# A fifth tile of source rows by matmul in one chunk of twelve

## The chip, the core and the metric

The kernel runs on one NeuronCore of a Trainium2 chip. A core has five engines that run their own instruction streams and meet at semaphores: TensorE (PE, matmuls and, separately shown, their weight loads PEld), VectorE (DVE), ScalarE (ACT), GpSimd (POOL) and SyncE (SP). SP, ACT and POOL also issue DMAs, each on queues of its own. The metric is the device time of one execution in microseconds; less is better.

## What is computed

A graph layer over 12500 nodes of 32 features and 400000 edges sorted by target. Node features are normalised and rectified; each edge takes its source's row, its target's row and its own 32 attributes through a small two-layer network; each node takes the maximum over its incoming edges.

```python
def _L0_gnn_ref(x, edge_index, edge_attr, W1, b1, W2, b2):
    rol, col = (edge_index[0], edge_index[1])
    e_feat = jnp.concatenate([x[rol], x[col], edge_attr], axis=-1)
    h = jax.nn.relu(e_feat @ W1 + b1)
    v = h @ W2 + b2
    x_cand = jax.ops.segment_max(v, col, num_segments=num_nodes)
    return jnp.maximum(x_cand, x[:, -v.shape[-1]:])

h = jnp.maximum(_layernorm(x, axis=-1), 0.0)
x = x + _L0_gnn_ref(h, edge_index, edge_attr_32, W1, b1, W2, b2)
```

## The kernel before

**Tiling.** The edges are cut into four stripes, each stripe into 196 chunks of 512 edges. A chunk is thus 4 x 512 edges, held as 16 groups of 128 source rows (K = 16). The main loop (L530) takes two chunks per turn, c and c + 1; while it finishes these it fetches the source rows of a = c + 2 and b = c + 3. One turn is called a pair below. On PE a pair starts with the matmuls `ph<-ht`, which multiply the transposed source rows of c and c + 1 by the first weights.

**Two ways to a source row.** Of the 16 groups of a chunk, 12 are gathered: `gather` (L148) issues one indirect DMA per group of 128 rows on POOL, out of `h_d` in memory, into a buffer `gh` that holds three groups; there are 24 such buffers, four to a chunk. The other four groups (MM = 4), in every chunk but the last, are picked by matmul out of a copy of all nodes kept on the core:

- The 98 nodes that each partition holds are cut into A1 = 7 groups of A0 = 14. `hs` holds each node's features in two parts, whose sum is the value.
- An edge's source index becomes a *key* (which partition and which group of 14) and a *place* within the 14. The keys are worked out once, at the start, from `src_mm` (L390 to L392) and written to `key_d` in memory. `load_keys` (L187) brings them back, broadcast to all partitions as `kb`, for two chunks by one DMA of 256 KB on ACT's queue.
- `one_hots` (L202, VectorE, five of the seven groups) and `one_hots_act` (L210, ScalarE, the other two) turn the keys into one-hot columns `hot`. `mask_of` (L219) makes the mask that selects the place.
- `tile(c, m)` (L227) does one group of 128 edges: 14 matmuls of 128 x 128 by 448 columns (7 groups, two parts each, L238) into a bank of PSUM `pv`, then on VectorE a multiply with the mask (L242) and a maximum over the 14 (L243) into `gm`. Two banks are called `pv`, and the second layer of the network uses the same two.

`to_features` (L245) transposes rows, gathered or picked, into `ht`: parts 0 to 3 take the four gathered buffers (L256), part J = 4 the four picked groups (L259).

**Order.** The order of the instructions on SP, PE, VectorE and ScalarE is that of the program text; an engine does not pass a waiting instruction. POOL's gathers wait only for a free buffer. A turn runs on PE as: `tile(a,0)`, `ph<-ht`, `tile(a,1)`, `tile(a,2)`, `ph<-ea` (edge attributes), the second layer into two `pv` banks (L569), `ph<-of` (target rows), the leaving matmuls of the chunk before (L486), `tile(a,3)`, the transposes of `leave_1` (L476), `tile(b,0)`, `leave_2` (L486), `tile(b,1)`, `leave_1`, `tile(b,2)`, `tile(b,3)`. [...] On VectorE the two scans of the turn (L576), which make the running maximum over edges of one target, stand just ahead of `tile(a,3)`'s multiply.

**Loads.** At the head of a turn the DMAs for later turns are issued. `load_keys(a + 2)` comes first. Then `load(k)` (L437) for k = c + 4 and c + 5; where k is a multiple of LOAD = 4 it brings four chunks at once: `ea` (1 MB, SP's queue), `db` (1 MB, target indices, ACT's queue) and `pb` (512 KB, penalties, ACT's queue, L445). On ACT these issues stand behind the last ScalarE work of the turn before (`wo`, L490) and ahead of `hid` (L552). Every so often `load_block` follows with `di` and `ends`.

## Time and profile before

| | |
|---|---|
| median of 12 runs | 3053.06 us (3049.39 to 3059.16) |
| the profiled execution | 3044.69 us, of which the span from the first to the last instruction is 3042.9 |
| matmuls of `tile` (L238) | 10920, 780 tiles of 14 |
| gathers (L154) | 2345, the first at 27.7 us, the last at 2995.9 |
| `ph<-ht`, first of the first and last pair | 86.9 and 2984.5 us |

The profile comes from one execution. A group line has the source line, engine, operation, tiles (`out<-in`) with shapes and count, then after the bar busy time in us, the mean ns of one, and the engine's idle time just ahead of them with what ended it. A timeline line has start, duration, engine, line, operation and tiles, and in brackets the idle time before it and its releaser. A wait line has who waited for whom, the total in us, how often, and the longest. A stretch line has the window, its length, the busy time of PE, PEld, VectorE, ScalarE and POOL, the granted clock of PE as a share of full, and the DMA engines' share and GB/s. A queue line has packets, MB and share of the DMA engines; q10 is ACT's queue. Matmuls are pipelined and their ends are modelled, so a busy PE is not PE at its peak, and of two runs of matmuls the distance between starts tells more than the durations.

### The profile page before, as it was taken

How to read it: one execution, taken by the hardware profiler on the slowest of the kernel's cores; microseconds unless marked ns; L12 is line 12 of the kernel's file. 1: busy time of each engine (PE TensorE's matmuls, PEld its weight loads, DVE VectorE, ACT ScalarE, POOL GpSimd, SP SyncE). 2: the span in 40 equal slices, each digit the busy share in tenths (PEclk: the TensorE clock that was granted, in tenths of full speed). 3: DMA queues.
4: the chain of work that ended last, by engine and by line, in shares of the span. 5: the costliest groups of instructions: out<-in, count | busy, mean ns of one | idle time of the engine just before them, and what ended most of it. 6: DMA issues, size and time to landing. Idle time of an engine off the chain costs nothing. (4 is left out here: it accounts for less than half of the span.)

```text
span 3042.9 us, 58825 instructions
## 1 busy us (share of the span) xinstructions
PE 2958.6 (97%) x21189; PEld 2322.5 (76%) x21189; DVE 2244.4 (74%) x3869; ACT 1089.1 (36%) x1795; POOL 2255.2 (74%) x2376
## 2 busy tenths in 40 slices
PE   5999999999999999999999999999999999999995
PEld 4677787777878787777787777777777877777773
DVE  6577777777777777777777777777777777777775
ACT  4242433333343433333333333333333333333331
POOL 6777777777777777777777777777777777777774
PEclk9899999999999999999999999999999999999998
DMA  6332233233323322332233223322322332233322
GB/s 246 73 85 64 62 82 78 62 65 83 73 59 83 76 63 66 79 75 65 61 82 78 59 67 85 70 63 65 86 71 59 70 84 68 63 67 84 67 58 71
DMA packets 194678, 229.58 MB, mean 75 GB/s; under 512 B 118333, under 2 KB 158797, under 8 KB 181582
## 3 DMA queue, kind: packets, MB, share of 16 engines
q10 hardware_dynamic: 32580, 110.55, 12.0%
q1 hardware_dynamic: 86762, 76.67, 10.4%
q0 software_dynamic: 75040, 38.57, 8.7%
q8 instruction: 167, 2.74, 0.4%
q14 instruction: 129, 1.06, 0.1%
HBM read 211.68 MB, written 13.85 MB: 74 GB/s over the span
## 5 line engine op out<-in xcount | busy, mean ns | idle before, releaser
L154 POOL DMA_INDIRECT gh<-h_d,src_i x2345 | 2235.1, 953 | 746.5 <-issue 532.4
L238 PE MATMUL pv<-hs,hot 128*128 128x448 f32 x10920 | 2358.1, 371 | 7.8 <-DVE sm L576 7.5
L238 PEld LDWEIGHTS pv<-hs,hot 128*128 128x128 f32 x10920 | 2014.5, 188 | 270.3 <-issue 70.8
L242 DVE TENSOR_TENSOR one<-pv,mask 128x448 f32<-128x448 f32 x780 | 483.3, 620 | 685.6 <-PE pv L238 685.0
L552 ACT ACTIVATE hid<-ph,wt 128x512 f32<-128x512 f32 x392 | 237.3, 689 | 1254.5 <-PE ph L500 1189.2
L207 DVE TENSOR_TENSOR hot<-kb,consts 128x1536 fp32r<-128x1536 f16 (+2 forms) x388 | 565.8, 1458 | 0.0
L243 DVE TENSOR_REDUCE gm<-one 128x32 f32<-128x448 f32 x780 | 483.7, 620 | 26.8
L217 ACT ACTIVATE hot<-away,ones 128x512 fp32r<-128x512 f32 x392 | 283.7, 724 | 244.2 <-issue 234.5
L216 ACT ACTIVATE away<-kb,key_n 128x512 f32<-128x512 f16 x392 | 277.9, 709 | 0.0
L576 DVE TENSOR_TENSOR_SCAN sm<-pb,sm,pv 128x512 f32<-128x512 bf16 x195 | 247.6, 1270 | 14.5 <-PE pv L569 4.2
L256 DVE STREAM_TRANSPOSE ht<-gh 128x96 f32<-128x96 f32 x782 | 210.3, 269 | 42.7 <-DMA gh<-h_d,src_i 42.1
L486 PEld LDWEIGHTS tr<-so,last 128*64 128x64 f32 x3136 | 107.6, 138 | 112.8 <-issue 77.9
L490 ACT ACTIVATE wo<-tr 128x64 f32<-128x64 f32 x196 | 43.8, 223 | 381.3 <-PE tr L486 352.6
L462 ACT ACTIVATE of<-db,below 128x512 f32<-128x512 int32 x196 | 141.8, 723 | 16.9 <-DMA db<-in_dst_ext 16.9
L463 ACT ACTIVATE of<-of,ones 128x512 f32<-128x512 f32 x196 | 142.0, 724 | 6.4
L486 PE MATMUL tr<-so,last 128*64 128x64 f32 x3136 | 134.8, 228 | 3.9 <-DVE so L478 3.9
L569 PE MATMUL pv<-hid,wt 64*32 64x512 f32 x1568 | 130.7, 601 | 5.0 <-DVE one L242 4.3
L468 DVE TENSOR_TENSOR last<-consts,at 128x512 f32<-128x512 f32 x196 | 129.9, 663 | 0.0
L478 DVE TENSOR_TENSOR so<-tr,wt 128x512 f32<-128x512 f32 x196 | 127.8, 652 | 2.1 <-PE tr L476 2.1
L500 PE MATMUL ph<-of,qw 32*64 32x512 f32 x1568 | 115.6, 619 | 13.9 <-DMA qw<-q_d 13.9
L476 PE MATMUL tr<-ident,sm 128*128 128x128 f32 x784 | 117.5, 272 | 1.5 <-DVE sm L576 0.8
L500 PE MATMUL ph<-ht,wt 32*64 32x512 f32 x1568 | 112.7, 613 | 0.2 <-DVE ht L262 0.2
(77 smaller groups left out, 552.7 us busy)
## 6 DMA issues: line engine op xcount, KB each, us to landing
ea<-in_edge_attr SPq DMA_DIRECT2D x49, 1024.0 KB
db<-in_dst_ext ACTq DMA_DIRECT2D x48, 1024.0 KB
gh<-h_d,src_i POOLq DMA_INDIRECT x2345
pb<-pen_d ACTq DMA_DIRECT2D x48, 512.0 KB
kb<-key_d ACTq DMA_DIRECT2D x95, 256.0 KB
qw<-q_d SPq DMA_DIRECT2D x784, 8.0 KB
top_d<-wo SPq DMA_DIRECT2D x784, 4.0 KB
top_d<-zero ACTq DMA_DIRECT2D x2, 1568.0 KB
```

The source lines that it names most:

```text
L154: nc.gpsimd.indirect_dma_start(out=parts[-1][:, i, :], out_offset=None, in_=h_d[:, :], in_offset=bass.IndirectOffsetOnAxis(ap=src_i[:, c, ...
L207: nc.vector.tensor_tensor(hot_of(c)[:, start:stop], keys[c][:, None, :].to_broadcast([P, n, MM * P]), key_ps[:, start:stop, None].to_broad ...
L216: nc.scalar.activation(away, keys[c], AF.Square, bias=key_n[:, k:k + 1])
L217: nc.scalar.activation(hot_of(c)[:, k], away, AF.Relu, bias=ones, scale=-1.0)
L238: nc.tensor.matmul(po, hot[:, k, e], hs[:, part, k].rearrange("p f a -> p (f a)"), start=(k == 0 and part == 0), stop=(k == A1 - 1 and par ...
L242: nc.vector.tensor_tensor(one, of_group, masks[c][:, m, None, :].to_broadcast([P, D, A0]), op=ALU.mult)
L243: nc.vector.tensor_reduce(mm_rows[c][:, m, :], one, axis=AX.X, op=ALU.max)
L256: nc.vector.transpose(ht[:, r].rearrange("p k e -> p (k e)"), gh[c][part][:, :r.stop - r.start].rearrange("p k f -> p (k f)"))
L486: nc.tensor.matmul(pw[g * 2 * W:(g + 1) * 2 * W], last[:, j, 2 * g:2 * g + 2].rearrange("p s w -> p (s w)"), so[:, j, g * 2 * D:(g + 1) * ...
L500: nc.tensor.matmul(ph[s][x * HID:(x + 1) * HID], w[g], e[g], start=start, stop=stop)
L552: nc.scalar.activation(hid[s], ph[s], AF.Relu, bias=b1c)
L576: nc.vector.tensor_tensor_scan(sm, loaded.pop(c + x)[2], pv[x], before, op0=ALU.add, op1=ALU.max)
```

## The change

`MORE = range(6, NCH - 12, 12)` names 15 chunks, 6, 18, ... 174. In these the group of rows K - MM - 1 = 11 is no longer gathered (11 gathers in place of 12, the fourth buffer `gh` holding two groups) but picked by matmul, as a fifth tile. It has keys of its own at the end of `key_d`, a load of its own on ACT's queue (`load_more`, 128 keys to 128 partitions, 32 KB), a one-hot of 7 x 128 columns made on VectorE alone (`hot_more`), a mask of its own, and a row buffer of its own. All chunks of `MORE` are even and so play the part of a. `load_more(a)` stands behind the loads at the head of the turn, `hot_more(a)` between the scans and `tile(a, 3)`, `tile_more(a)` behind the last gathered part's transpose. The matmuls and the two VectorE instructions of `tile` move into `pick`, which both kinds of tile call. `places` works out the fifth tiles' places once, in its first call.

```diff
+MORE = range(6, NCH - 12, 12)
...
+    place_m = const.tile([P, len(MORE)], F32, name="place_m")
...
+    def gathers(c):
+        return min(K - MM * (c in MMC) - (c in MORE), (SE - c * C) // D)
+
     def gather(c):
-        n = min(K - MM * (c in MMC), (SE - c * C) // D)
+        n = gathers(c)
...
     def places(start, stop):
 
-        se = src_i[:, MMC.start + start:MMC.start + stop, K - MM:]
-        pk = place_k.rearrange("p (c m) -> p c m", m=MM)[:, start:stop]
-        group(pk, se)
-        nc.vector.scalar_tensor_tensor(pk, pk, -float(A0), se, op0=ALU.mult, op1=ALU.add)
+        more = src_i[:, MORE.start:MORE.stop:MORE.step, K - MM - 1]
+        for pk, se in ((place_k.rearrange("p (c m) -> p c m", m=MM)[:, start:stop],
+                        src_i[:, MMC.start + start:MMC.start + stop, K - MM:]),
+                       (place_m, more))[:1 + (start == 0)]:
+            group(pk, se)
+            nc.vector.scalar_tensor_tensor(pk, pk, -float(A0), se, op0=ALU.mult, op1=ALU.add)
...
     def tile(c, m):
 
-        if c not in MMC:
-            return
-        if m == 0:
-            mm_rows[c] = early.tile([P, MM, D], F32, name="gm", bufs=6)
-        hot = hots[c]
-        e = slice(m * P, (m + 1) * P)
+        if c in MMC:
+            if m == 0:
+                mm_rows[c] = early.tile([P, MM, D], F32, name="gm", bufs=6)
+            pick(hots[c][:, :, m * P:(m + 1) * P], masks[c][:, m], mm_rows[c][:, m, :])
+
+    def load_more(c):
+        if c in MORE:
+            kb = early.tile([P, P], F16, name="kb_more", bufs=1)
+            nc.scalar.dma_start(kb, ap(key_d, (len(MMC) * MM + MORE.index(c)) * P, [[0, P], [1, P]]))
+            keys_more[c] = kb
+
+    def hot_more(c):
+        if c in MORE:
+            hot = early.tile([P, A1, P], F32R, name="hot_more", bufs=1)
+            nc.vector.tensor_tensor(hot, keys_more[c][:, None, :].to_broadcast([P, A1, P]),
+                                    key_ps[:, :, None].to_broadcast([P, A1, P]), op=ALU.is_equal)
+            mask = early.tile([P, A0], F32, name="mask_more", bufs=1)
+            k = MORE.index(c)
+            nc.vector.tensor_tensor(mask, place_ps, place_m[:, k:k + 1].to_broadcast([P, A0]), op=ALU.is_equal)
+            keys_more[c] = hot, mask
+
+    def tile_more(c):
+
+        if c in MORE:
+            rows = early.tile([P, D], F32, name="gm_more", bufs=1)
+            pick(*keys_more.pop(c), rows)
+            nc.vector.transpose(hts[c][:, K - MM - 1], rows)
+
+    def pick(hot, mask, rows):
         po = early_ps.tile([P, C], F32, name="pv", bufs=2)[:, :D * A0]
...
-                nc.tensor.matmul(po, hot[:, k, e], hs[:, part, k].rearrange("p f a -> p (f a)"),
+                nc.tensor.matmul(po, hot[:, k], hs[:, part, k].rearrange("p f a -> p (f a)"),
...
-        nc.vector.tensor_tensor(one, of_group, masks[c][:, m, None, :].to_broadcast([P, D, A0]), op=ALU.mult)
-        nc.vector.tensor_reduce(mm_rows[c][:, m, :], one, axis=AX.X, op=ALU.max)
+        nc.vector.tensor_tensor(one, of_group, mask[:, None, :].to_broadcast([P, D, A0]), op=ALU.mult)
+        nc.vector.tensor_reduce(rows, one, axis=AX.X, op=ALU.max)
...
-            nc.vector.transpose(ht[:, n:].rearrange("p k e -> p (k e)"),
+            nc.vector.transpose(ht[:, K - MM:].rearrange("p k e -> p (k e)"),
                                 mm_rows.pop(c).rearrange("p k f -> p (k f)"))
...
-        key = pool.tile([P, len(MMC) * MM], F32, name="key")
-        key16 = pool.tile([P, len(MMC) * MM], F16, name="key16")
+        key = pool.tile([P, len(MMC) * MM + len(MORE)], F32, name="key")
+        key16 = pool.tile([P, len(MMC) * MM + len(MORE)], F16, name="key16")
...
+            load_more(a)
             tile(a, 0)
             to_features(a, 0)
...
+            hot_more(a)
             tile(a, 3)
             one_hots_act(a + 2)
             to_features(a, 3)
+            tile_more(a)
             to_features(a, J)
```

`key_d`, `src_mm` and its tile `sp` grow by 15 x 128 keys; the host lays these behind the others.

More of the change, by code (lines that the diff above doesn't have):

```diff
@@ L94, in gnn_kernel @@
     top_d = [dram.tile([NP, D], F32, name=f"top_d{k}") for k in range(2)]
-    key_d = dram.tile([len(MMC) * MM * P], F16, name="key_d")
+    key_d = dram.tile([(len(MMC) * MM + len(MORE)) * P], F16, name="key_d")
     acc_d = dram.tile([NP, D], F32, name="acc_d")
@@ L171, in gnn_kernel @@
     hts = {}
+    keys_more = {}
     loaded_b, ats = {}, {}
@@ L251, in to_features @@
         ht = hts[c]
-        n = min(K - MM * (c in MMC), (SE - c * C) // D)
+        n = gathers(c)
         if part < J:
@@ L289, in gnn_kernel @@
     with tc.tile_pool(name="nodes", bufs=1) as pool, tc.tile_pool(name="nodes_ps", bufs=2, space=PSUM) as ps:
-        sp = pool.tile([P, len(MMC) * MM], I32, name="sp")
+        sp = pool.tile([P, len(MMC) * MM + len(MORE)], I32, name="sp")
         nc.scalar.dma_start(sp, src_mm)
@@ L725 @@
     sc = np.ascontiguousarray(sp.reshape(NS, NCH, K, D).transpose(1, 2, 0, 3).reshape(NCH, K, P))
-    sm = sc[MMC.start:MMC.stop, K - MM:]
+    sm = np.concatenate([sc[MMC.start:MMC.stop, K - MM:].reshape(-1),
+                         sc[MORE.start:MORE.stop:MORE.step, K - MM - 1].reshape(-1)])
     w1, w2 = np.asarray(L0_gnn_W1), np.asarray(L0_gnn_W2)
@@ L741 @@
         "src": np.ascontiguousarray(sc.transpose(2, 0, 1).reshape(P, NCH * K)),
-        "src_mm": np.ascontiguousarray(sm.reshape(P, len(MMC) * MM)),
+        "src_mm": sm.reshape(P, len(MMC) * MM + len(MORE)),
         "src_t": sp.reshape(NS, TS, P),
```

## The prediction

> **What bounds the kernel now.** I read the busy shares and the groups of instructions first.

> ```profile
> PE 2958.6 (97%) x21189; PEld 2322.5 (76%) x21189; DVE 2244.4 (74%) x3869; ACT 1089.1 (36%) x1795; POOL 2255.2 (74%) x2376
> ...
> L154 POOL DMA_INDIRECT gh<-h_d,src_i x2345 | 2235.1, 953 | 746.5 <-issue 532.4
> L238 PE MATMUL pv<-hs,hot 128*128 128x448 f32 x10920 | 2358.1, 371 | 7.8 <-DVE sm L576 7.5
> ```

> PE looks like the bound at 97%, POOL at 74% does not. But a gather of 953 ns is followed by a gap of 0.30 us "issue" nearly every time, so POOL is in truth never free: its 2235 us and its 746 us of gaps fill the span from the first gather to the last. Two engines are full, and the question is which one gives the pace, and when. For that I took the busy time by stretch, cut at the first matmul of a pair of chunks (`ph<-ht`): 32 pairs in the first row, 62 in the second.

> ```profile
> 153.10:1106.10 953.00, 953.00 (x6913) 754.76 (x6912) 722.49 (x1255) 348.26 (x576) 715.85 (x753) 1.00 0.32 72
> 1106.10:2984.50 1878.40, 1866.28 (x13393) 1464.04 (x13392) 1397.25 (x2413) 674.78 (x1116) 1413.93 (x1486) 1.00 0.30 70
> ```

> Up to 1106 us PE is busy all the time and a pair takes 953.0/32 = 29.78 us. After that a pair takes 1878.4/62 = 30.30 us and PE has holes. What VectorE waits for says why (200 to 1000 us, then 1100 to 2990 us):

> ```profile
> DVE one L242 <- PE pv L238: 181.7, 151, 1.9
> ...
> DVE one L242 <- PE pv L238: 416.1, 353, 2.6
> DVE ht L256 <- DMA gh<-h_d,src_i: 42.1, 54, 2.1
> ```

> Early it waits for matmuls alone; late it waits for gathers too. POOL starts ahead (some 30 us between a gather's end and the transpose that reads it), loses half a microsecond per pair to PE, and from 1106 us on the lead is used up. So **PE sets the first third and POOL the rest**, and they differ by only 0.52 us per pair. An edit that gives work from POOL to PE can gain at most what POOL costs over PE, 62 x 0.52 = 32 us.

> **The change, part by part.** There are 15 such chunks (6, 18, ... 174).

> *Gathers removed*: 15. One costs 1878.4/1486 = 1.264 us of POOL, so POOL has 19.0 us less. Six pairs now hold 143 gathers, 180.8 us of POOL, against 6 x 29.78 + 2.95 = 181.6 us of PE (the 2.95 follows). POOL no longer falls behind, the lead of 30 us is never used up, and the whole 32 us of waiting for gathers goes: **-32**.

> *Matmuls added*: 14 per tile. The rows below give 42 of them from 323.80 to the next matmul at 332.56, 2.92 us per tile, and a lone 14 from 320.47 to 323.44, 2.97; I take 2.95. Nothing hides them, since PE is the pace once POOL is quick enough: 15 x 2.95 = **+44.3**.

> *VectorE's part*: the one-hot of 7 x 128 = 896 elements. 1024 take 1182 ns and 1536 take 1726 (L207), so 1.06 ns an element and 1.05 us; mask below the 0.20 us of L222; multiply and reduce 0.62 each (L242, L243); a transpose of 32 columns under the 0.27 of L256. One-hot and mask (1.25) fall into the 1.90 us in which VectorE waits before the multiply at 346.40, the rest runs under the next matmuls as it does for other tiles: 0 while that cover holds. The four small instructions on `place_m` and the wider key are at most +0.8 us at the start, once.

> *The keys' load*: this is the part I give most weight. It is one DMA of 32 KB on ACT's queue, issued behind whatever `load(k)` put there. A fifth-tile chunk is a = 6 + 12i, so c = 4 + 12i, and there `load` of chunk c + 4 = 8 + 12i, a multiple of 4, puts db and pb (1.5 MB) on the same queue in the same iteration, every time. The timeline of one such pair before the change (c = 16), and what ACT's queue (q10) moved from 319 to 334, 334 to 344.5 and 344.5 to 349.3 us:

> ```profile
> 320.47 3.13 PE L238 MATMUL pv<-hs,hot 128*128 128x448 f32 x14
> 320.65 0.33 ACTq L192 DMA_DIRECT2D kb<-key_d  x1
> 321.01 0.56 ACTq L444 DMA_DIRECT2D db<-in_dst_ext  x1
> 321.67 0.51 ACTq L445 DMA_DIRECT2D pb<-pen_d  x1
> ...
> 323.80 8.83 PE L238 MATMUL pv<-hs,hot 128*128 128x448 f32 x42
> ...
> 332.56 1.11 PE L500 MATMUL ph<-ht,wt 32*64 32x512 f32 x16
> ...
> 341.86 2.64 DVE L576 TENSOR_TENSOR_SCAN sm<-pb,sm,pv 128x512 f32<-128x512 bf16 x2
> ...
> 343.25 3.12 PE L238 MATMUL pv<-hs,hot 128*128 128x448 f32 x14
> 346.00 0.56 PEld L476 LDWEIGHTS tr<-ident,sm 128*128 128x128 f32 x4
> ...
> 346.40 0.63 DVE L242 TENSOR_TENSOR one<-pv,mask 128x448 f32<-128x448 f32 x1 [1.90 <-PE pv L238]
> ```

> ```profile
> q10 hardware_dynamic: 223, 0.91, 22.5%
> ...
> q10 hardware_dynamic: 100, 0.59, 16.7%
> ...
> q10 hardware_dynamic: 85, 0.33, 17.0%
> ```

> 0.91 + 0.59 + 0.33 = 1.83 MB is the kb, db and pb issued near 321 us (1792 KB). They go in turn: by packet size, kb's end first, then db's, then pb's, the last at 349.2. The keys would be issued at 322.2 and stand behind pb. VectorE wants them when the scans end, at 344.5; they come after 349.2. Over the 15 pairs concerned, the queue's last packet of that load ends 14.0 to 18.7 us after the pair's first matmul, mean 16.7; the fourth tile's matmuls end 13.6 us after it. Add 0.4 us for the 32 KB (0.33 MB in 4.8 us is 69 KB per us), 1.05 for the one-hot, 0.1 to hand over: PE stands still for 16.7 + 1.55 - 13.6 = 4.65 us. Behind the waiting one-hot on VectorE are the mask, the fourth tile's multiply and reduce and everything after; behind the tile's first matmul on PE are the transposes of `leave_1` and tile (b,0). All of it moves together and none of it is made up, PE having no holes: 15 x 4.65 = **+70**. Bounds: all as the earliest (14.0) 29, all as the latest 100.

> *The clock*. PE has not stood still for that long since the start. There it did three times, 5.1, 9.3 and 3.46 us, and after each the granted clock was half for 6.8, 13.7 and 6.8 us; the last of them (the clock is the third column from the right):

> ```profile
> 85.40:99.00 13.60, 11.61 (x94) 7.17 (x92) 10.04 (x15) 8.38 (x13) 10.25 (x12) 1.00 0.46 137
> 99.00:105.90 6.90, 5.43 (x14) 3.06 (x14) 0.00 (x0) 0.00 (x0) 5.11 (x6) 0.51 0.41 105
> ```

> Holes up to 1.25 us later on left it at 1.00. 4.65 us is nearest to the 5.1 and 3.46. Half clock for 6.8 us, about 1 of it in the hole itself, makes matmuls slower by 1.7 to 1.8 times, a loss of 2.5 us; I give each hole 8 chances in 10: 15 x 2.0 = **+30**. Bounds 0 and 46 (every hole, 3.1 each). [...]

> **Sum**: -32 + 44.3 + 0.8 + 70 + 30 = +113 us on the profiled execution's 3042.9 us of span (3044.7 with what lies around it). That execution is 8 us quicker than the median of the runs, 3053.06. I put the difference on the median: 3053 + 113 = **3166 us**. With the low bounds -32 + 44.3 + 0.8 + 29 = 42, so 3095; with the high ones 100 and 46, 159, so 3212.

> **Rivals.**
> 1. *Late keys, clock stays up*: 113 - 30 = 83, 3136 us. For it: only three cases of a drop, all at the start. Against it: the shortest of them was shorter than these holes.
> 2. *Keys in time*: the queue lets a small DMA pass, or its load ends earlier. Then -32 + 44.3 + 0.8 = 13, 3066 us. Against it: pb's packets follow db's in turn, and not one of the 15 loads ended before the scans.
> 3. *Faster*: PE takes the tile into its holes and POOL's 19.0 us come off, 3034 us. It decides if a tile costs PE under (32 - 19)/15 = 0.87 us with keys in time. Against it: 2.92 measured, and before 1106 us there are no holes.
> 4. *Worse*: holes long enough for 13.7 us of half clock, as after the 9.3 us. Another 3 us each, 45 in all, 3211 us.

> That the change doesn't do what it says I exclude: 11 gathers are issued, the fourth transpose covers rows 9 and 10, the tile's row 11.

> **Chances.** Forecast 0.65, rival 1 0.20, rival 2 0.08, rival 3 0.02, rival 4 0.05. The predicted time is the forecast's. The range 3095 to 3212 takes the bounds of the stall and the clock, holds rival 1 and half of rival 4, and leaves out rivals 2 and 3. A measurement here can tell 0.2%, 6 us, from no change. Faster by more: 0.02 (rival 3). Within it: 0.02, a rival 2 in which 7 of the 13 us are hidden. Slower: 0.96.

> **What would show it.** VectorE waits before the new one-hot for `kb_more`, about 15 times 5 us; holes of 4 to 5 us on PE before the fifth tile's matmuls and half clock after most of them; no waits of `ht` for gathers; pairs of 29.8 us without a fifth tile, and about 39 us with one. The forecast is wrong if the keys land before the scans end (then pairs of 32.7 us), or if VectorE still waits for gathers late in the run.

## The result, and the profile after

The changed kernel takes 3174.29 us in the median of 8 runs (3162.42 to 3178.70), the kernel before 3052.73 (34 runs): a ratio of 1.0393 with a 95% interval of 1.038 to 1.0406, some 121 us slower. The profiled execution has a span of 3161.1 us against 3042.9.

The page of the changed kernel: busy time by engine, the gathers, and the matmuls of the fifth tiles.

```profile
PE 3015.6 (95%) x21399; PEld 2386.1 (75%) x21399; DVE 2277.0 (72%) x3948; ACT 1089.1 (34%) x1795; POOL 2242.4 (71%) x2361
...
L159 POOL DMA_INDIRECT gh<-h_d,src_i x2330 | 2221.8, 954 | 804.3 <-issue 568.9
...
L269 PE MATMUL pv<-hs,hot_more 128*128 128x448 f32 x210 | 73.1, 526 | 74.7 <-DVE mask_more L255 74.7
```

There are 15 gathers fewer and 210 matmuls more. The new matmuls last 526 ns each where those of the other tiles last 371, and PE stands idle for 74.7 us ahead of them. VectorE's waits in the changed kernel:

```profile
DVE one L273 <- PE pv L269: 722.0, 555, 20.3
DVE hot_more L251 <- DMA kb_more<-key_d: 84.2, 15, 8.5
...
DVE ht L287 <- DMA gh<-h_d,src_i: 1.9, 2, 1.5
```

It waits for the fifth tile's keys 15 times out of 15, 84.2 us in all, 8.5 at most; the wait for gathers (42.1 us before) has shrunk to 1.9. One pair shows how that comes about. This is the timeline of the turn c = 16, with what ACT's queue moved from 332 to 344.4, 344.4 to 356.4 and 356.4 to 363 us.

```profile
332.60 0.33 ACTq L200 DMA_DIRECT2D kb<-key_d  x1
332.97 0.56 ACTq L475 DMA_DIRECT2D db<-in_dst_ext  x1
333.62 0.52 ACTq L476 DMA_DIRECT2D pb<-pen_d  x1
...
335.91 0.32 ACTq L245 DMA_DIRECT2D kb_more<-key_d  x1
...
353.78 2.64 DVE L608 TENSOR_TENSOR_SCAN sm<-pb,sm,pv 128x512 f32<-128x512 bf16 x2
...
355.17 3.11 PE L269 MATMUL pv<-hs,hot 128*128 128x448 f32 x14
...
363.00 1.09 DVE L251 TENSOR_TENSOR hot_more<-kb_more,consts 128x896 fp32r<-128x896 f16 x1 [6.57 <-DMA kb_more<-key_d]
364.00 0.17 DVE L255 TENSOR_TENSOR mask_more<-consts,place_m 128x14 f32<-128x14 f32 x1
...
364.23 5.19 PE L269 MATMUL pv<-hs,hot_more 128*128 128x448 f32 x14 [5.94 <-DVE mask_more L255]
...
369.26 0.60 PE L507 MATMUL tr<-ident,sm 128*128 128x128 f32 x4
```

```profile
q10 hardware_dynamic: 315, 0.80, 24.9%
...
q10 hardware_dynamic: 77, 0.57, 17.7%
...
q10 hardware_dynamic: 160, 0.50, 18.8%
```

0.80 + 0.57 + 0.50 = 1.87 MB is kb, db, pb and the 32 KB of keys. A DMA of 32 KB issued at 335.91 has landed at 363.00, 27 us later, when the last of the megabyte and a half ahead of it has gone. It doesn't stand behind them as a whole: going by size and time of the packets on q10 (256 bytes are the keys, 8 KB db, 4 KB pb), 96 of its 128 packets go from 336.9 to 338.1, while db's have only begun, and the last 32 from 361.0 to 362.2, with the last of pb's at 362.1. It is 96 and 32 in each of the 15 turns. The one-hot needs all of them. The scans are over at 356.42; VectorE idles 6.57 us, PE 5.94. Then 14 matmuls take 369.26 - 364.23 = 5.03 us (that is up to the next matmul's start) where the fourth tile's took some 2.95. The granted clock around the holes of two such pairs tells why (third column from the right):

```profile
362.00:368.80 6.80, 4.57 (x12) 4.13 (x13) 2.47 (x5) 0.00 (x0) 5.28 (x6) 0.50 0.11 20
...
2061.90:2065.30 3.40, 3.30 (x9) 2.98 (x10) 1.34 (x4) 0.00 (x0) 2.48 (x4) 0.50 0.10 18
```

All 15 holes (stretches in which PE stands still ahead of the fifth tile), 2.38 to 7.87 us long, were followed by half clock, for 3.4 us (8 of them), 6.8 (6) or 10.2 (1). Between the first and the last fifth tile the clock was full everywhere else.

### The profile page after: what moved, and what is told of

It is laid out like the page before. It is cut to its first block, busy times and chain, and to the rows that moved or that the text cites. A ratio compares the mean times of both kernels' runs of the same rounds, so it can differ in the third digit from the quotient of the medians.

```text
span 3161.1 us, 59320 instructions
## 1 busy us (share of the span) xinstructions
PE 3015.6 (95%) x21399; PEld 2386.1 (75%) x21399; DVE 2277.0 (72%) x3948; ACT 1089.1 (34%) x1795; POOL 2242.4 (71%) x2361
## 3 DMA queue, kind: packets, MB, share of 16 engines
q14 instruction: 130, 1.06, 0.1%
## 5 line engine op out<-in xcount | busy, mean ns | idle before, releaser
L269 PEld LDWEIGHTS pv<-hs,hot 128*128 128x128 f32 x10920 | 2016.6, 188 | 259.3 <-issue 70.6
L225 ACT ACTIVATE hot<-away,ones 128x512 fp32r<-128x512 f32 x392 | 283.3, 723 | 235.5 <-issue 225.8
L287 DVE STREAM_TRANSPOSE ht<-gh 128x96 f32<-128x96 f32 (+1 forms) x782 | 209.4, 268 | 1.9 <-DMA gh<-h_d,src_i 1.9
L269 PE MATMUL pv<-hs,hot_more 128*128 128x448 f32 x210 | 73.1, 526 | 74.7 <-DVE mask_more L255 74.7
L269 PEld LDWEIGHTS pv<-hs,hot_more 128*128 128x128 f32 x210 | 60.5, 296 | 86.5 <-issue 79.8
```

The source lines that it names most:

```text
L225: nc.scalar.activation(hot_of(c)[:, k], away, AF.Relu, bias=ones, scale=-1.0)
L269: nc.tensor.matmul(po, hot[:, k], hs[:, part, k].rearrange("p f a -> p (f a)"), start=(k == 0 and part == 0), stop=(k == A1 - 1 and part = ...
L287: nc.vector.transpose(ht[:, r].rearrange("p k e -> p (k e)"), gh[c][part][:, :r.stop - r.start].rearrange("p k f -> p (k f)"))
```

## The experiments

All use the changed kernel as their base. The kernels of a series were compared with the kernel before on the same chip. Chips differed: on three of six the kernel before took 3059 to 3064 us, on the other three 4146 to 4207. What the latter say is told in a part of its own; the numbers of the next three parts are from chips of the first kind.

**Keys ahead of the large loads.** One call moves up by a few lines.

```diff
             load_keys(a + 2)
+            load_more(a)
             for k in range(c + AHEAD, min(c + AHEAD + 2, NCH)):
                 load(k)
...
-            load_more(a)
             tile(a, 0)
```

> Keys issued ahead of db and pb, a third time, since both earlier series fell on chips where the kernel before takes over 4140 us. Where it takes about 3053 us: theory (late keys) 3066 us, no wait of the one-hot for its keys, no hole on PE ahead of the fifth tile; rival (the tile's own work) near 3174 us.

Measured: 3061.44 us against 3059.17 for the kernel before, 1.0008 (0.9996 to 1.0019). VectorE's waits in this kernel no longer have the keys, and PE starts the fifth tile without a hole:

```profile
DVE one L273 <- PE pv L269: 701.1, 571, 20.0
DVE acc L657 <- DMA part<-top_d: 10.8, 3, 8.5
...
DVE ht L287 <- DMA gh<-h_d,src_i: 2.8, 3, 1.5
```

```profile
347.01 2.64 DVE L608 TENSOR_TENSOR_SCAN sm<-pb,sm,pv 128x512 f32<-128x512 bf16 x2
349.57 1.06 DVE L251 TENSOR_TENSOR hot_more<-kb_more,consts 128x896 fp32r<-128x896 f16 x1
```

```profile
348.40 3.12 PE L269 MATMUL pv<-hs,hot 128*128 128x448 f32 x14
351.36 3.00 PE L269 MATMUL pv<-hs,hot_more 128*128 128x448 f32 x14
354.20 0.60 PE L507 MATMUL tr<-ident,sm 128*128 128x128 f32 x4
```

VectorE hardly waits for gathers here either (2.8 us). The one-hot follows the scans at once and the fifth tile the fourth. Its 14 matmuls take 354.20 - 351.36 = 2.84 us; over the 15 tiles it is 2.83 each, 42.5 us. The pairs with a fifth tile take 32.56 us, the others 29.77, and the clock is 1.00 from the first of them to the last. So the place of one 32 KB load accounts for nearly all of the 121 us: same matmuls, same one-hots, same order on PE and VectorE. The rival, that the tile's own work costs it, falls.

**Gathers left out, nothing in their place.** The fifth group of rows is set to zero; keys, one-hot and matmuls are gone.

```diff
-            pick(*keys_more.pop(c), rows)
+            nc.vector.memset(rows, 0.0)
...
-            load_more(a)
...
-            hot_more(a)
```

> The fifteen gathers are left out and the fifth group of rows is set to zero, no tile in its place, asked again. Where the kernel before takes about 3055 us: theory (POOL sets the pace from 1106 us on) 19 us less, 3036 us, 0.994 of before; rival (PE sets it throughout) no change.

Measured: 3046.25 us against 3064.09, 0.994 (0.9924 to 0.9957), 18 us less, where 15 x 1.264 = 19 us was POOL's price. PE's work is the same, and so is its own pace (a pair before the first long one takes 29.7 us in either profile), so PE alone does not set the pace of the kernel before, and the rival falls. Putting the fifth tiles' matmuls on top, as the kernel with the keys ahead does, raises the ratio from 0.994 to 1.0008, some 21 us for 42.5 us of matmuls, so about half of that work cost nothing. One thing had been expected otherwise (in the first series, below): that VectorE's wait for gathers would halve. It begins later (the first long pair is the 45th in place of the 37th), but comes to the same sum, 42.9 us after 42.1 (1100 to 2990 us):

```profile
DVE one L273 <- PE pv L269: 409.8, 350, 2.8
DVE ht L287 <- DMA gh<-h_d,src_i: 42.9, 51, 3.7
```

The pairs say the same: 95 of them take 30.08 us in the mean, after 30.12. So the two profiles don't show where the 18 us came from. The profile before is of an execution of 3044.69 us, and on the chip of this experiment the kernel before takes 3064.09; no trace of it was kept from there, and whether its waits were longer on that chip is open.

**The hole filled.** Late keys as in the change, but PE runs 22 matmuls of the fourth tile's shape ahead of the fifth's. They write the bank that the fifth tile's first matmul clears.

```diff
+FILL = 22
...
-            pick(*keys_more.pop(c), rows)
+            pick(*keys_more.pop(c), rows, hots[c][:, :, 3 * P:])
...
         po = early_ps.tile([P, C], F32, name="pv", bufs=2)[:, :D * A0]
+        if other is not None:
+            for k in range(FILL):
+                nc.tensor.matmul(po, other[:, k % A1], hs[:, 0, k % A1].rearrange("p f a -> p (f a)"),
+                                 start=True, stop=True)
```

> Late keys as in the change, 22 matmuls put into the wait, asked again. Where the kernel before takes about 3053 us: theory (the clock drops because PE stands still) clock 1.00 in nearly all of the fifteen places and 3152 us, 1.032 of before; rival (the half clock has another cause or costs nothing) 3181 us, 1.042 of before.

Measured: 3167.10 us against 3058.79, 1.0355 (1.0333 to 1.0377), between the two. By time alone this settles nothing, since the keys came later in the profiled execution: VectorE waited 105.8 us for them, not 84.2, and PE still had holes.

```profile
DVE hot_more L252 <- DMA kb_more<-key_d: 105.8, 15, 9.1
```

The trace settles it. Of the 15 places, 7 had half clock and 8 did not. The holes left ahead of the 7 were 2.05, 2.17, 2.94, 3.33, 3.36, 3.66 and 3.89 us; ahead of the 8 they were 2.16, 1.59, 1.28, 1.02, 0.48, 0.25, 0.19 and none. In one of the 8, the turn c = 16 again, 22 matmuls run to 364.81, the hole is 1.02 us, and the tile has its full pace:

```profile
360.18 4.63 PE L270 MATMUL pv<-hs,hot 128*128 128x448 f32 x22
365.83 3.10 PE L274 MATMUL pv<-hs,hot_more 128*128 128x448 f32 x14 [1.02 <-DVE hot_more L252]
368.77 0.60 PE L512 MATMUL tr<-ident,sm 128*128 128x128 f32 x4
```

The same keys are as late, and with PE kept busy the tile takes 2.94 us in place of 5.03. Over all, the 15 tiles take 55.2 us here, 70.6 in the changed kernel, 42.5 with the keys ahead. So the half clock follows from the hole: in the two traces it came after every hole of 2.05 us and more but the one of 2.16 (more in the last section). The rival falls.

**On chips of the other kind.** Two series and one later run fell on chips on which the kernel before takes 4206 us (first series), 4146 (second) and 4207 (the last line). The edit of the second kernel below is `MORE = range(8, NCH - 12, 12)`, of the last `MORE = range(8, NCH - 12, 24)`.

| | ratio to the kernel before | interval |
|---|---|---|
| keys ahead, first series | 0.9991 | 0.9975 to 1.0007 |
| chunks 8, 20, ... 176 | 0.9979 | 0.9965 to 0.9992 |
| gathers only, first series | 0.9942 | 0.9923 to 0.9961 |
| hole filled, first series | 1.0190 | 1.0165 to 1.0214 |
| keys ahead, second series | 1.0057 | 1.0035 to 1.0080 |
| gathers only, second series | 0.9949 | 0.9934 to 0.9965 |
| hole filled, second series | 1.0250 | 1.0227 to 1.0272 |
| eight chunks, second series | 1.0017 | 1.0005 to 1.0028 |
| eight chunks, later run | 0.9995 | 0.9984 to 1.0007 |

What was expected of the first series, in this order:

> The fifth tile's keys are issued just ahead of db and pb on the same queue in the same turn; nothing else differs from the changed kernel. Theory (the keys stand behind 1.5 MB, PE waits for them and its clock drops): no wait of the new one-hot for its keys, no hole, clock 1.00, and of the 121 us lost only PE's own work less the saved gather waits stays: 44 - 32 + 1 = 13 us, 3066 us. Rival (the cost is the fifth tile itself, its one-hot ahead of the fourth tile's multiply and its place on PE): the time stays near 3174 us.

> The fifteen chunks are 8, 20, ... 176 in place of 6, 18, ... 174, so that their keys are loaded in turns that bring no db and pb; the order within a turn is that of the change. Theory: the keys stand behind 256 KB or, where a block is loaded too, some 540 KB at most, and land well before the scans end: 3066 us, as with the keys issued ahead. Rival (a load that is issued ahead of tile (a,0) in the same turn is too late anyway, whatever stands before it): near 3174 us, or in between where only a part of the wait goes.

> The fifteen gathers are left out and nothing comes in their place: the fifth group of rows is set to zero, without keys, one-hot or matmuls. Theory (POOL sets the pace over the run as a whole from 1106 us on): 15 x 1.264 = 19 us less, 3034 us, and VectorE waits for gathers about half as much and from later on. Rival (PE sets the pace throughout): no change, 3053 us.

> Keys as late as in the change, but 22 matmuls of the fourth tile's shape, which write the bank that the fifth tile's first matmul clears, run on PE while it would wait (4.6 us). Theory (the clock drops because PE stands still): the clock stays at 1.00 in nearly all of the fifteen places; the wait itself stays, and holes shorter than 4.6 us are made longer by 7 us in sum, so 3174 - 29 + 7 = 3152 us. Rival (the half clock has another cause, or costs next to nothing since the tile waits anyway): 3174 + 7 = 3181 us.

Of the second, in which the first three kernels below (keys ahead, gathers only, hole filled) ran again because the kernel before had taken 4206 us in the first, and of the two runs with eight chunks:

> [...] Where the kernel before takes about 3053 us: theory (late keys) 3066 us, no wait for the keys, no hole on PE, clock 1.00; rival (the tile's own work costs it) near 3174 us.

> [...] Where the kernel before takes about 3053 us: theory (POOL sets the pace from 1106 us on) 3034 us; rival (PE sets it throughout) 3053 us.

> [...] Where the kernel before takes about 3053 us: theory (the clock drops because PE stands still) clock 1.00 in nearly all of the fifteen places and 3152 us; rival (the half clock has another cause or costs nothing) 3181 us.

> Eight chunks in place of fifteen: 8, 32, ... 176, whose turns bring no db and pb. PE's own pace over the run is 3053 - 32 = 3021 us, plus 8 x 2.95 gives 3045; POOL's pace is 3053 - 8 x 1.264 = 3043. Theory (two paces, the slower one counts, keys in time): 3045 to 3047 us, 0.2% to 0.3% less than before. Rival (the two paces do not share out so evenly, since every second pair's landings are late): 3050 us or more, no difference from before.

> Eight chunks in place of fifteen (8, 32, ... 176), in turns that bring no db and pb, asked again. Where the kernel before takes about 3055 us: theory (two paces, the slower one counts, keys in time) PE's pace 3055 - 32 + 8 x 2.83 = 3046 and POOL's 3055 - 8 x 1.264 = 3045, so some 3047 us, 0.997 of before. Rival (the late landings of every second pair keep the gather waits): 3055 us, no difference.

These chips can't tell late keys from keys in time: a pair takes about 41 us there, the scans end later after the loads' issue (in hole filled of the second series the first of the 15 one-hots starts at 264.6 us, 29.1 us after its keys' issue at 235.5; in the changed kernel's turn above the scans end 20.5 us after it), and even the kernel with the late order has no wait for `kb_more` in its trace. That is why filling the hole is a plain loss there, of 71 to 88 us over the keys ahead (15 x 22 matmuls of 0.21 us are 69). Nor can they tell POOL's pace: gathers only saved 23 and 20 us here too (4206.16 to 4183.54, 4146.31 to 4126.20), though POOL has time to spare (in gathers only of the first series it is busy for 1531 of the 2807 us from 153 to 2960, where the kernel before has 2111 on a chip of the first kind). What that saving comes from is open, so a saving of this size does not by itself prove that POOL is the pace. Not shown on a chip of the first kind are the chunks shifted by two, and the eight chunks, which by the two paces should have taken 0.3% less than the kernel before. On the chips of the other kind the eight gave 1.0017 and 0.9995. No version was shown to be quicker than the kernel before and keep its computation on the chips of the first kind.

## Why the prediction was right

The time was forecast at 3166 us and came to 3174; the sum at +113 us, and the two profiled spans differ by 118.2. Term by term:

| | forecast, us | profile after, us |
|---|---|---|
| waits for gathers gone | -32 | -35 |
| the tiles' matmuls | +44.3 | +42.5 |
| PE standing still for the keys | +70 | +74.7 |
| half clock | +30 | +31 |
| start and end | +0.8 | +5 |

The first is 95 pairs by the difference between 30.117 us (their mean before) and 29.751 (mean of the 80 without a fifth tile). The second is the pace with the keys in time. The half clock is the 70.6 us that the tiles took less 42.5, and 2.7 us in what follows them: the 15 pairs took 39.61 us, 148 more than 15 of 29.75, of which 74.7 and 70.6 are accounted for. The last is the difference in the first and last pairs and the stretches outside them, in single executions.

*Which engine sets the pace.* Right as far as it was tried: gathers alone out gave 18 us of 19, and with PE's work added the waits for gathers went. That POOL is full at 74% busy was read from the constant gap of 0.30 us behind each gather. The profile of gathers only, with waits as long as before, does not fit in with this, and the saving on the chips of the other kind has no explanation.

*The queue.* Right in size and in its effect: all 15 came late, by 5.6 us of VectorE's time on average. The mechanism holds for a quarter of the load: three quarters of its packets (96 of 128) passed db and pb, as rival 2 had it, but the last quarter (32) went when the forecast said, and that one counts. The one experiment that changes nothing but the load's place takes the cost away.

*The clock.* Right in sum by luck, since two errors offset each other: 8 drops in 10 were forecast, of 6.8 us each; it was 15 of 15, and more than half of them lasted 3.4 us. Rival 1 had the clock stay up; it did not once. The forecast went by three holes at the start of the profile before, the shortest 3.46 us; the runs showed drops after holes from 2.05 us on.

*Keys in time.* Rival 2's price of 13 us rested on one profile's gather waits. By the profiled spans it is 12.9 us (3055.8 after 3042.9), but the second is of an execution 8 us quicker than its median. Beside the kernel before on one chip, the kernel with keys in time was 1.0008 of it, -1 to +6 us. By the same sum the gather waits that the change removes and the matmuls that it adds would nearly cancel there; whether that chip's waits were larger than the 32 us of the one profile was not tried.

*Start.* Forecast at 0.8 us; whether the 5 us there belong to the change is open.

## What to carry to other kernels

A new load that is small and soon needed can cost the time of whatever stands ahead of it on its queue, even if only a part of it has to wait: here 32 KB behind 1.5 MB had all arrived 27 us after the issue, and its place a few lines further up was worth 4%. Where one engine is the pace, count a stall on it twice, once for the time it stands and once for the clock it loses: here 15 holes of 2.4 to 7.9 us, 75 us in sum, cost another 31 us at half clock. Two engines that are both full are a balance; moving work between them can gain no more than the one costs over the other, 32 us here, and a profile's busy share does not show that an engine with a gap behind each instruction is full.

## What the runs showed of the hardware that was not expected

```profile
2437.20:2440.60 3.40, 1.63 (x8) 1.52 (x9) 2.47 (x5) 1.75 (x3) 0.46 (x1) 1.00 0.09 15
2440.60:2444.00 3.40, 3.40 (x21) 3.12 (x20) 1.81 (x5) 0.00 (x0) 2.78 (x3) 1.00 0.10 12
2816.10:2819.50 3.40, 1.45 (x7) 1.36 (x8) 2.47 (x5) 1.92 (x3) 0.10 (x1) 1.00 0.09 13
2819.50:2822.90 3.40, 3.40 (x13) 2.94 (x12) 0.45 (x1) 0.00 (x0) 2.60 (x3) 0.50 0.07 12
```

Behind these holes the half clock ended with the first piece in which PE was idle for 0.50 us or less, and went on after those with 0.76 or more; it lasted one, two or three pieces (3.4, 6.8 or 10.2 us). So two holes of nearly the same length, 2.16 and 2.17 us, differed by where they fell: full clock after the one, half after the other. At the start of the changed kernel the same figures do not hold: half clock at 41.17 us came after a piece with 1.49 us idle, and it went on after two pieces in which PE was busy throughout (82.13 to 85.54 and 102.61 to 106.00). They describe the holes ahead of the fifth tile in these two traces, and why they lie where they do was not shown.

Chips differ by more than a third in the time of the same program: the kernel before takes 3059 to 3064 us on three of the six, 4146 to 4207 on the other three. On the chips where the kernel before takes over 4140 us, two groups of 16 small matmuls take much longer: `ph<-ea` (edge attributes, each 32 rows by 64 columns of the array) 4.1 to 5.1 us in the median of a trace, against 1.04, and `pv<-hid` (64 by 32) 3.8 to 4.4, against 1.05. It is not the shape alone, since `ph<-ht` is 32 by 64 as well and keeps its median of 1.04, and a tile of 14 matmuls of 128 by 128 takes 3.03 us, against 2.97. PE also stands still more often there (in gathers only of the first series 246 times ahead of `pv<-hs` matmuls with no releaser in the trace, 167.5 us in sum; the kernel before on a chip of the first kind has PE idle for 12.1 us in all from 153.1 to 2984.5), and the clock halves about once per pair: 96 times for 771 us in all in gathers only (150 to 4110 us), once for 3 us in the same kernel on a chip of the first kind. At half clock `ph<-of` takes 1.94 us, at full clock 1.04. This is PE in the gathers-only kernel on such a chip, all three groups at half clock, and in the kernel before on one of the first kind:

```profile
1504.33 4.15 PE L531 MATMUL ph<-ea,wt 32*64 32x512 f32 x16 [0.74 <-ACT hid L583]
1508.41 3.28 PE L600 MATMUL pv<-hid,wt 64*32 64x512 f32 x16
1511.62 2.01 PE L531 MATMUL ph<-of,qw 32*64 32x512 f32 x16
```

```profile
1508.20 1.11 PE L500 MATMUL ph<-ea,wt 32*64 32x512 f32 x16
1509.25 1.12 PE L569 MATMUL pv<-hid,wt 64*32 64x512 f32 x16
1510.30 1.11 PE L500 MATMUL ph<-of,qw 32*64 32x512 f32 x16
```

The half clock accounts for a part, but `ph<-ea` took a median of 3.12 us in gathers only even at full clock (29 of 98 times). Why is open. It is a reason to compare only with the kernel before on the same chip.
